# A long convolution and a mixture of experts on one core: x copied into the output in memory, the shared expert added by adding transfers, and shared and routed work in one ordered region

## The chip, the cores and the metric

The kernel runs on one core of a Trainium2 chip. A core has five engines that each work through a queue of their own: TensorE (PE, matrix products, with its weight loads listed apart as PEld), VectorE (DVE), ScalarE (ACT), GpSimd (POOL) and SyncE (SP, which here only issues transfers and waits). Transfers run on 16 DMA engines beside them, and an engine may issue transfers from its own queue. The metric is the time of one execution on the device in microseconds (us); of several runs the median is given. The trace gives spans of each instruction, and the page drawn from it also gives the clock that TensorE was granted.

## The reference

Two layers, all in single precision. A state-space layer makes a kernel of 512 taps for each of 32 heads, convolves each head of x (128 batch rows, 32 heads, 512 positions) with it causally, adds x times D and masks by the row's length. Its output goes to a mixture of experts with one shared expert, and x is added to the sum.

```python
def _L0_cond_ref(u, log_dt, C, log_A_real, A_imag, D, length):
    # K (32, 512) = 2 * Re(sum over 64 states of Ct * exp(dtA * l))
    K = _get_kernel(log_dt, C, log_A_real, A_imag, Lq)
    y = causal_convolution(u, K)          # written with rfft / irfft
    y = y + u * D[:, None]
    mask = (jnp.arange(Lq)[None, :] < length[:, None]).astype(u.dtype)
    return y * mask[:, None, :]

def _L0_ffn_ref(hidden_states, gate_w, bias, Wg, Wu, Wd, Sg, Su, Sd):
    x = hidden_states.reshape(-1, 512)                   # 4096 tokens
    scores = jax.nn.sigmoid(x @ gate_w.T) + bias         # 16 experts
    topk_w, topk_idx = jax.lax.top_k(scores, 4)
    topk_w = topk_w / (jnp.sum(topk_w, axis=-1, keepdims=True) + 1e-20)
    cw = jnp.sum(jax.nn.one_hot(topk_idx, 16) * topk_w[..., None], axis=1)
    z = silu(einsum('th,eih->eti', x, Wg)) * einsum('th,eih->eti', x, Wu)
    out = einsum('eti,ehi->th', z * cw.T[:, :, None], Wd)        # I = 256
    return out + silu(x @ Sg.T) * (x @ Su.T) @ Sd.T

x = x + ffn(cond(x, ..., lengths))      # lengths lie between 78 and 453
```

## The kernel before

The work runs in four stages. The first two are put in order by a scheduler, which decides from dependences and its own costs in which order each engine's queue gets its instructions; the last two are written out in the order in which they are to be issued.

*Making the convolution's kernels (0 to about 24 us).* Heads are handled in pairs, and the 16 pairs in four chunks, of 2, 4, 4 and 6 pairs. For a chunk, `waves` builds sines on ACT and exponentials on DVE and POOL: POOL makes `wv`, and DVE turns it into an exponential by a series (`exp_parts`, L244 to L251, on tiles `wv`, `wk`, `wq` of 192 columns for the second chunk). `kernels` then multiplies factors into `f_r`, `f_i`, `gg_r`, `gg_i` (DVE and POOL), a small product `pk` on PE sums over states, DVE adds D (`krow`, L392), SP writes `krow` to a scratch `kd` in memory (L399), and `kernel_strip` reads it back as `strip`, a Toeplitz matrix of 4 heads by 512 columns (L409; 1 MB, and for the first block four pieces of 256 KB). Only the first chunk also needs the tiles ct_r and ct_i, which all later ones use.

*Convolution (first product at 26.62 us, last gate product at 153.8).* There are NB = 8 blocks `tb` of HB = 4 heads. For each head `convolve` multiplies x's transposed block `xt` with the strip into `py` (four products, L512), DVE evacuates it under the length mask into `yb` (L519), PE transposes it into `pt` while ordering batch rows by length (L522), and ACT copies it to `yh` and to `yT` (L524 to L526). After each block a transfer in ACT's queue stores `yb` as rows of `y_rows` (L826), `gates` multiplies `yh` with the gate's weights (`pg`, L545), and after every second block `route` computes the routing on DVE; its last step is a product `cw_ps` on PE (L603), a copy to `cw_o` on ACT and a store (L606). The chunk of a later block is made two blocks ahead in program order, its strip one block ahead. SP loads `xt` for the next block and, at the start, the lengths (`len_col`, `len_row`).

*Shared expert (153.8 to 327.2 us).* `unit_step(u)` handles NU = 8 units of 512 tokens: 16 rows of neighbouring length by 32 heads. It computes g (`up`, L889), SiLU on ACT (L948), u (L889) and z on DVE (L951), twice, with 1 to 4 products of 128 positions as the lengths need; then `down` (L915) for the unit before, in four quarters of 128 tokens. POOL `fetch`es the rows of x for a quarter by an indirect transfer into `xg` (L903), DVE adds `o` to `xg` (L922), and POOL puts the rows into `out` by an indirect transfer (L924). Between these, `next(making)` takes one step at a time of `slots`, a generator that makes the tables of the routed tiles: counts (step 1), `nu_b` (2), `marks` and others (3), `pos`, `slot` and others (4), load tables (5), and then 16 groups of 8 one-hot pairs on DVE (`rows`, `cols`, L778 and L779) that PE sums into `pa` (L767). `unit_step(8)` has only the last `down`s. Once the tables are there, SP loads experts' weights into a ring of R = 8 places (`store`, 1.5 MB each, L840).

*Routed tiles (to the end).* Up to 143 tiles of 128 tokens of one expert. `turn_of(step)` gathers the tokens of a tile four ahead (POOL, L854), transposes them (`tokens`, L997, copied on ACT to `yt`, L1003), multiplies g and u (`inner`, L1029), makes z (L1040, L1041), transposes it (`turn`, L1047, L1050), multiplies down (`outer`, L1055), copies to `ob` (L1064, in the buffers `xg`) and adds the rows to `out` by an adding indirect transfer on POOL (L1065). `order` makes SP wait for all adds of the expert before when a new expert begins, since the same row may be added to.

Of the kernel before, what the change touches and what calls it, by code (L numbers as in the profile page):

```python
# [28 lines left out]
F32 = mybir.dt.float32  # L29
# [45 lines left out]
def ssm_moe_kernel(  # L75
# [459 lines left out]
    pgs = {}  # L535
# [17 lines left out]
    def route(rb):  # L553
# [46 lines left out]
        nc.vector.tensor_mul(cw, s, over_e(free))  # L600

        cw_ps = ps_m.tile([P, nh * E], F32, tag="m", name=f"cw_ps{rb}")
        nc.tensor.matmul(cw_ps, lhsT=to_row, rhs=flat(cw), start=True, stop=True)  # L603
        cw_o = stile("cw_o")
        nc.scalar.copy(flat(cw_o), cw_ps)
        nc.sync.dma_start(out=y_bh[:, hs, L:], in_=cw_o)  # L606
# [209 lines left out]
    for tb in range(NB):  # L816
        yb = yp.tile([P, HB, L], F32, tag="yb", name=f"yb{tb}")
        x_next = load_xt(tb + 1) if tb + 1 < NB else None
        for q in range(HB):
            convolve(tb, q, xb, yb)  # L820
            if tb * HB + q in chunk_at:
                c0, n = chunk_at[tb * HB + q]
                kernels(c0, n, *waves(c0, n, 0)[0])
            if q == 0 and tb + 1 < NB:
                kernel_strip(tb + 1)
        nc.scalar.dma_start(out=y_bh[:, tb * HB : (tb + 1) * HB, :L], in_=yb)  # L826
        gates(tb)
        if tb % RB == RB - 1:
            route(tb // RB)
        xb = x_next  # L830
# [47 lines left out]
    xg = homes(fp, "xg", [P, L], 6)  # L878
# [20 lines left out]
    def rows_of(u, q):  # L899
        return bass.IndirectOffsetOnAxis(ap=unit_rows[:, u, q : q + 1], axis=0)  # L900

    def fetch(u, q):
        nc.gpsimd.indirect_dma_start(  # L903
            out=at(xg, u * (TU // P) + q),
            out_offset=None,
            in_=x_rows,
            in_offset=rows_of(u, q),
        )

    def down(u, q):  # L910
        n = u * (TU // P) + q
        po, xq = at(p_o, n), at(xg, n)
        for it in range(IT):
            c0 = WD + it * L
            nc.tensor.matmul(  # L915
                po,
                lhsT=at(zu, u)[:, it, q * P : (q + 1) * P],
                rhs=w_sh[:, c0 : c0 + L],
                start=(it == 0),
                stop=(it == IT - 1),  # L920
            )
        nc.vector.tensor_add(xq, po, xq)  # L922
        nc.gpsimd.nop()
        put = nc.gpsimd.indirect_dma_start(  # L924
            out=out, out_offset=rows_of(u, q), in_=xq, in_offset=None
        )
        for other in adds:
            tc.declare_no_dep(put.ins, other.ins, reason="other rows")
        adds.append(put)
# [8 lines left out]
    def unit_step(u):  # L938
# [3 lines left out]
        if u < NU:  # L942
            fetch(u, 0)
            fetch(u, 1)
            k_us[u] = nc.tensor.value_load(k_u[0:1, u : u + 1], min_val=1, max_val=KT)
            for it in range(IT):
                up(u, it, p_g, 0)
                nc.scalar.activation(sgu[it], p_g[it], AF.Silu)  # L948
                next(making, None)
                up(u, it, p_u, I)  # L950
                nc.vector.tensor_mul(at(zu, u)[:, it, :], sgu[it], p_u[it])  # L951
                next(making, None)
        if u > 0:
# [31 lines left out]
    obs = xg[:3]  # L985
# [5 lines left out]
    def tokens(t):  # L991
# [9 lines left out]
        else:  # L1001
# [5 lines left out]
            texp[:, t : t + 1],  # L1007
# [11 lines left out]
    def registers(t):  # L1019
        w0s[t] = nc.tensor.value_load(  # L1020
            woff[0:1, t : t + 1], min_val=0, max_val=(R - 1) * WSZ
        )
        k_ts[t] = nc.tensor.value_load(ntk[0:1, t : t + 1], min_val=1, max_val=KT)
# [28 lines left out]
    def outer(t):  # L1052
        po = at(p_o, t)
        for it in range(IT):
# [12 lines left out]
            out_offset=bass.IndirectOffsetOnAxis(ap=put[:, t : t + 1], axis=0),  # L1067
# [9 lines left out]
    def order(t):  # L1077


        new = nc.sync.value_load(fresh[0:1, t : t + 1], min_val=0, max_val=1)  # L1080
        with tc.If(new > 0):
            wait = nc.sync.nop()
            for other in adds:
                dep(wait, other, "the rows they add to")
        marks[t] = nc.sync.nop()

    with tc.manual_schedule(engines=None):
        registers(0)

        def turn_of(step):  # L1090
# [26 lines left out]
        for step in range(NT_MIN + 2):  # L1117
            turn_of(step)

        def rest(step):  # L1120

            if step == NT + 2:
                return
            _, (some,) = nc.values_load_multi_w_load_instructions(
                full[0:1, step - 2 : step - 1], min_val=0, max_val=1
# [57 lines left out]
```

## Time and profile before

| | |
|---|---|
| Three runs | 965.4, 962.52, 962.6 us; median 962.6 |
| The profiled execution | 962.73 us, span of the trace 961.0 us |
| Mean granted TensorE clock | 0.986 |
| TensorE busy | 905.0 us, 94% of the span |
| VectorE, ScalarE, GpSimd busy | 426.6, 185.3, 431.2 us |
| First product of the convolution | 26.62 us |
| Last gate product / first product of the shared expert | 153.8 us |
| Last `down` of the shared expert ends | 327.2 us |

Busy times of different engines overlap, so they do not add up to the span: an engine that is busy 44% of the time costs nothing unless another waits for it. The table of windows gives, for a stretch of the span, the busy time of PE, PEld, DVE, ACT, POOL and SP with the number of instructions, then the granted clock, the mean busy share of the DMA engines and their GB/s. In the timeline a line gives start and length in us, the engine (SPq is SP's DMA queue), the line of the kernel, the operation with output and inputs, how many were taken together, and in brackets what ended an idle time before it.

### The profile page before, as it was taken

Reading aid. Unit: us, or ns where it says so; the run is one execution under the profiler, and the core shown is the slowest. Engines: PE = TensorE matmul, PEld = TensorE weight load, DVE = VectorE, ACT = ScalarE, POOL = GpSimd, SP = SyncE. Lnnn points to the kernel's source line nnn. Section 1 sums busy time; section 2 is a strip of 40 time slices with the busy share of each in tenths; the row PEclk is TensorE's granted clock in tenths of the full one; section 3 lists DMA queues with packets and bytes.
Section 4 is the critical chain, followed back from the end, with each engine's and each line's share of the span. In section 5 each row is a group of like instructions: output and inputs, shape, how many; then the busy total and the mean of one; then the engine's idle time right before and its main releaser. Section 6 shows DMA issues by size and latency. Waiting matters only on the chain.

```text
span 961.0 us, 14800 instructions
## 1 busy us (share of the span) xinstructions
PE 905.0 (94%) x3088; PEld 467.7 (49%) x3088; DVE 426.6 (44%) x1438; ACT 185.3 (19%) x367; POOL 431.2 (45%) x396
## 2 busy tenths in 40 slices
PE   0899998989998999999999999999999999999995
PEld 0567775434444444444444444444444544444442
DVE  7835555778762223342334233423433323334332
ACT  1133332000001012221222112211222212222221
POOL 3210002033455545564556555655555445556644
PEclk9999998999999999999999999999999999999998
DMA  4466653164456766777667766765766656667765
GB/s 160 138 214 197 205 175 114 43 251 146 165 197 192 252 157 113 126 141 160 113 119 139 166 113 116 140 107 110 123 125 113 113 90 113 113 116 138 131 111 104
DMA packets 53649, 135.96 MB, mean 141 GB/s; under 512 B 12400, under 2 KB 12560, under 8 KB 50960
## 3 DMA queue, kind: packets, MB, share of 16 engines
q0 software_dynamic: 35616, 89.77, 47.8%
q1 hardware_dynamic: 13680, 36.15, 11.2%
q10 hardware_dynamic: 4224, 8.39, 2.3%
q8 instruction: 72, 1.18, 0.5%
q14 instruction: 57, 0.47, 0.1%
HBM read 288.08 MB, written 52.25 MB: 354 GB/s over the span
## 4 chain that ended last, share of the span: by engine, by line
PE 85%; DVE 10%; issue 2%; another core or an unknown queue 1%; POOL 1%; ACT 0%; DMA 0%; SPq 0%; DVEq 0%; POOLq 0%
PE g L1029 34%; PE o L1055 24%; PE py L512 7%; PE m L997 4%; PE o L915 4%; PE u L1047 3%; PE pg L545 3%; PE u L889 2%; DVE cols L779 2%; PE pt L522 2%; PE g L889 2%; DVE rows L778 1%; DVE z L951 1%; DVE wq L251 1%
## 5 line engine op out<-in xcount | busy, mean ns | idle before, releaser
L1029 PE MATMUL g<-store,yt 128*128 x742 | 344.7, 598 | 4.4 <-ACT yt L1003 2.9
L1065 POOL DMA_INDIRECT out<-xg,put x134 | 212.1, 1583 | 238.5 <-DVE junk L1004 205.8
L1055 PE MATMUL o<-store,zT 128*128 x536 | 252.1, 593 | 0.0
L1041 DVE SCALAR_TENSOR_TENSOR zt<-g,wt,sgt 128x256 f32<-128x256 f32 x135 | 65.3, 483 | 290.2 <-ACT sgt L1040 284.0
L1029 PEld LDWEIGHTS g<-store,yt 128*128 128x128 f32 x742 | 130.9, 191 | 122.4 <-issue 118.0
L1055 PEld LDWEIGHTS o<-store,zT 128*128 128x128 f32 x536 | 101.4, 190 | 129.0 <-issue 124.6
L854 POOL DMA_INDIRECT yg<-y_rows,get x140 | 138.7, 991 | 42.6 <-issue 29.5
L1064 DVE COPY xg<-o 128x512 f32<-128x512 f32 x134 | 92.6, 691 | 108.8 <-PE o L1055 107.7
L1003 ACT COPY yt<-m 128x512 f32<-128x512 f32 x136 | 79.5, 585 | 234.8 <-PE m L997 220.7
L1040 ACT ACTIVATE sgt<-g 128x256 f32<-128x256 f32 x135 | 51.7, 383 | 273.4 <-PE g L1029 231.4
L512 PE MATMUL py<-strip,xt 128*128 128x512 f32 (+3 forms) x256 | 82.8, 460 | 4.9 <-DMA strip<-kd 4.9
L997 PEld LDWEIGHTS m<-ident,yg 128*128 128x128 f32 x373 | 48.6, 141 | 72.6 <-issue 72.6
L903 POOL DMA_INDIRECT xg<-in_x,unit_rows x32 | 31.1, 973 | 108.4 <-DVE sig_k L245 98.0
L924 POOL DMA_INDIRECT out<-xg,unit_rows x32 | 31.5, 984 | 93.3 <-DVE xg L922 86.0
L915 PE MATMUL o<-store,z 128*128 128x512 f32 x128 | 58.9, 609 | 6.1 <-DVE xg L922 6.1
L997 PE MATMUL m<-ident,yg 128*128 128x128 f32 x373 | 63.1, 273 | 1.2 <-issue 1.1
L1050 DVE COPY zT<-u 128x256 f32<-128x256 f32 x134 | 56.2, 419 | 0.1
L512 PEld LDWEIGHTS py<-strip,xt 128*128 128x128 f32 x256 | 44.0, 201 | 19.0 <-issue 8.3
L1047 PE MATMUL u<-ident,zt 128*128 128x128 f32 x268 | 51.3, 273 | 0.9 <-DVE zt L1041 0.9
L889 PE MATMUL g<-store 128*128 128x512 f32 x92 | 44.9, 625 | 0.0
L889 PE MATMUL u<-store 128*128 128x512 f32 x92 | 42.9, 601 | 0.7 <-issue 0.7
L915 PEld LDWEIGHTS o<-store,z 128*128 128x128 f32 x128 | 24.2, 195 | 37.1 <-issue 27.1
(267 smaller groups left out, 569.0 us busy)
## 6 DMA issues: line engine op xcount, KB each, us to landing
store<-in_w_all SPq DMA_DIRECT2D x143, 1536.0 KB
xt<-in_x_t SPq DMA_DIRECT2D x8, 1024.0 KB
y_rows<-yb ACTq DMA_DIRECT2D x8, 1024.0 KB
strip<-kd SPq DMA_DIRECT2D x7, 1024.0 KB
yg<-y_rows,get POOLq DMA_INDIRECT x140
out<-xg,put POOLq DMA_INDIRECT x134
strip<-kd SPq DMA_DIRECT2D x4, 256.0 KB
xg<-in_x,unit_rows POOLq DMA_INDIRECT x32
```

The source lines that it names most:

```text
L512: nc.tensor.matmul(py[:, : L - jt * P], lhsT=xt[:, jt, q, :], rhs=strip[tb][:, q, jt * P :], start=(jt == 0), stop=(jt == KT - 1),)
L854: nc.gpsimd.indirect_dma_start(out=at(yg, t), out_offset=None, in_=y_rows[:, :], in_offset=bass.IndirectOffsetOnAxis(ap=made["get"][:, t : ...
L889: nc.tensor.matmul(ps[it], lhsT=w_sh[:, c0 : c0 + P], rhs=yT[:, u, kt, :, :].rearrange("p h b -> p (h b)"), start=(kt == KT - n), stop=(kt ...
L915: nc.tensor.matmul(po, lhsT=at(zu, u)[:, it, q * P : (q + 1) * P], rhs=w_sh[:, c0 : c0 + L], start=(it == 0), stop=(it == IT - 1),)
L997: nc.tensor.transpose(pt[:, q, :], at(yg, t)[:, q * P : (q + 1) * P], ident)
L1003: nc.scalar.copy(at(yt, t), pt)
L1029: mm = nc.tensor.matmul(pgu, lhsT=at(yt, t)[:, q, :], rhs=ring_flat[:, bass.ds(w0s[t] + q * 2 * I, 2 * I)], start=(q == KT - n), stop=(q = ...
L1041: nc.vector.scalar_tensor_tensor(at(zs, t), pgu[:, I:], at(wts, t), sg, ALU.mult, ALU.mult)
L1047: nc.tensor.transpose(at(p_z, t)[:, it, :], at(zs, t)[:, it * P : (it + 1) * P], ident)
L1055: mm = nc.tensor.matmul(po, lhsT=at(zts, t)[:, it, :], rhs=ring_flat[:, bass.ds(w0s[t] + WD + it * L, L)], start=(it == 0), stop=(it == IT ...
L1064: nc.vector.tensor_copy(ob, po)
L1065: add = nc.gpsimd.indirect_dma_start(out=out, out_offset=bass.IndirectOffsetOnAxis(ap=put[:, t : t + 1], axis=0), in_=ob, in_offset=None, ...
```

## The change

x is no longer fetched and added in the shared expert. Instead eight transfers from memory to memory, one per block of the convolution and 1 MB each, copy x into `out` in ACT's queue (two added lines after the store of `yb`). `fetch` is gone; `down` copies its result to `ob` on ACT and adds it to `out` by an adding indirect transfer. The last step of `route` becomes `weights_out`; for the last pair of blocks it is called in `unit_step(0)` behind the products of that unit. `next(making)` is called after each z and after the second and fourth quarter of `down`, in unit 0 too, which has no `down`; before, it was called after each g and each z. Shared and routed stages stand in one ordered region, with `turn_of(0)` ahead of `unit_step(8)`. The routed tiles use the six `ob` buffers where they used three of `xg`, and their tables are looked up in `made` when they are wanted. Products and their shapes are the same in both kernels.

```diff
@@ -598,12 +598,19 @@
         nc.vector.reciprocal(free, tot)
         cw = stile("cw")
         nc.vector.tensor_mul(cw, s, over_e(free))
-
+        cws[rb] = cw
+
+    def weights_out(rb):
+
+
+        nh = RB * HB
         cw_ps = ps_m.tile([P, nh * E], F32, tag="m", name=f"cw_ps{rb}")
-        nc.tensor.matmul(cw_ps, lhsT=to_row, rhs=flat(cw), start=True, stop=True)
-        cw_o = stile("cw_o")
-        nc.scalar.copy(flat(cw_o), cw_ps)
-        nc.sync.dma_start(out=y_bh[:, hs, L:], in_=cw_o)
+        nc.tensor.matmul(
+            cw_ps, lhsT=to_row, rhs=cws[rb].rearrange("p h e -> p (h e)"), start=True, stop=True
+        )
+        cw_o = sp.tile([P, nh, E], F32, tag="cw_o", name=f"cw_o{rb}")
+        nc.scalar.copy(cw_o.rearrange("p h e -> p (h e)"), cw_ps)
+        nc.sync.dma_start(out=y_bh[:, rb * nh : (rb + 1) * nh, L:], in_=cw_o)
 
 
     def ctile(name, shape, dtype=F32):
@@ -824,9 +831,14 @@
             if q == 0 and tb + 1 < NB:
                 kernel_strip(tb + 1)
         nc.scalar.dma_start(out=y_bh[:, tb * HB : (tb + 1) * HB, :L], in_=yb)
+
+        own = slice(tb * P * HB, (tb + 1) * P * HB)
+        nc.scalar.dma_start(out=out[own, :], in_=x_rows[own, :])
         gates(tb)
         if tb % RB == RB - 1:
             route(tb // RB)
+            if tb + 1 < NB:
+                weights_out(tb // RB)
         xb = x_next
     conv.close()
     cst = ctx.enter_context(tc.tile_pool(name="cst", bufs=1))
@@ -875,7 +887,7 @@
 
     zu = homes(fp, "z", [P, IT, TU], 2)
     sgu = homes(fp, "sg", [P, TU], 2)
-    xg = homes(fp, "xg", [P, L], 6)
+    obs = homes(fp, "ob", [P, L], 6)
     p_g, p_u = homes(ps_g, "g", [P, TU], 2), homes(ps_u, "u", [P, TU], 2)
     p_o = homes(ps_o, "o", [P, L], 2)
     k_us, adds, loads = {}, [], []
@@ -896,20 +908,9 @@
 
         by_tiles(k_us[u], products)
 
-    def rows_of(u, q):
-        return bass.IndirectOffsetOnAxis(ap=unit_rows[:, u, q : q + 1], axis=0)
-
-    def fetch(u, q):
-        nc.gpsimd.indirect_dma_start(
-            out=at(xg, u * (TU // P) + q),
-            out_offset=None,
-            in_=x_rows,
-            in_offset=rows_of(u, q),
-        )
-
     def down(u, q):
         n = u * (TU // P) + q
-        po, xq = at(p_o, n), at(xg, n)
+        po, ob = at(p_o, n), at(obs, n)
         for it in range(IT):
             c0 = WD + it * L
             nc.tensor.matmul(
@@ -919,14 +920,18 @@
                 start=(it == 0),
                 stop=(it == IT - 1),
             )
-        nc.vector.tensor_add(xq, po, xq)
+        nc.scalar.copy(ob, po)
         nc.gpsimd.nop()
-        put = nc.gpsimd.indirect_dma_start(
-            out=out, out_offset=rows_of(u, q), in_=xq, in_offset=None
+        add = nc.gpsimd.indirect_dma_start(
+            out=out,
+            out_offset=bass.IndirectOffsetOnAxis(ap=unit_rows[:, u, q : q + 1], axis=0),
+            in_=ob,
+            in_offset=None,
+            compute_op=ALU.add,
         )
         for other in adds:
-            tc.declare_no_dep(put.ins, other.ins, reason="other rows")
-        adds.append(put)
+            tc.declare_no_dep(add.ins, other.ins, reason="other rows")
+        adds.append(add)
 
     def free_after(j):
 
@@ -940,22 +945,20 @@
 
         nonlocal gathered
         if u < NU:
-            fetch(u, 0)
-            fetch(u, 1)
             k_us[u] = nc.tensor.value_load(k_u[0:1, u : u + 1], min_val=1, max_val=KT)
             for it in range(IT):
                 up(u, it, p_g, 0)
                 nc.scalar.activation(sgu[it], p_g[it], AF.Silu)
-                next(making, None)
                 up(u, it, p_u, I)
                 nc.vector.tensor_mul(at(zu, u)[:, it, :], sgu[it], p_u[it])
                 next(making, None)
-        if u > 0:
-            for q in range(TU // P):
+        if u == 0:
+            weights_out(NB // RB - 1)
+        for q in range(TU // P):
+            if u > 0:
                 down(u - 1, q)
-        if u < NU:
-            fetch(u, 2)
-            fetch(u, 3)
+            if q % 2 == 1:
+                next(making, None)
         while "get" in made and gathered < AHEAD:
             gather(gathered)
             gathered += 1
@@ -964,15 +967,6 @@
             e = nc.sync.value_load(made["lexp0"][0:1, j : j + 1], min_val=0, max_val=E - 1)
             loads.append(load_expert(e, ring_flat[:, j * WSZ : (j + 1) * WSZ]))
 
-    with tc.manual_schedule(engines=None):
-        for u in range(NU + 1):
-            unit_step(u)
-    for _ in making:
-        pass
-    put, texp, woff, load, loff, lexp, ntk, fresh, full = (
-        made[t] for t in "put texp woff load loff lexp ntk fresh full".split()
-    )
-
 
     w0s, k_ts = {}, {}
 
@@ -982,7 +976,6 @@
     sgs = homes(gp, "sgt", [P, I], 2)
     zs = homes(gp, "zt", [P, I], 2)
     zts = homes(gp, "zT", [P, IT, P], 2)
-    obs = xg[:3]
     p_t, p_gu = homes(ps_m, "m", [P, KT, P], 2), homes(ps_g, "g", [P, 2 * I], 2)
     p_z = homes(ps_u, "u", [P, IT, P], 2)
 
...
@@ -1085,6 +1078,10 @@
         marks[t] = nc.sync.nop()
 
     with tc.manual_schedule(engines=None):
+        for u in range(NU):
+            unit_step(u)
+        for _ in making:
+            pass
         registers(0)
 
         def turn_of(step):
@@ -1106,15 +1103,17 @@
             if 1 <= step < NT:
 
                 t = step - 1
-                e = nc.sync.value_load(lexp[0:1, t : t + 1], min_val=0, max_val=E - 1)
-                to = nc.sync.value_load(loff[0:1, t : t + 1], min_val=0, max_val=(R - 1) * WSZ)
-                go = nc.sync.value_load(load[0:1, t : t + 1], min_val=0, max_val=1)
+                e = nc.sync.value_load(made["lexp"][0:1, t : t + 1], min_val=0, max_val=E - 1)
+                to = nc.sync.value_load(made["loff"][0:1, t : t + 1], min_val=0, max_val=(R - 1) * WSZ)
+                go = nc.sync.value_load(made["load"][0:1, t : t + 1], min_val=0, max_val=1)
                 ld = load_expert(e, ring_flat[:, bass.ds(to, WSZ)], go)
                 for other in loads:
                     tc.declare_no_dep(ld.ins, other.ins, reason="another place of the ring")
                 loads.append(ld)
 
-        for step in range(NT_MIN + 2):
+        turn_of(0)
+        unit_step(NU)
+        for step in range(1, NT_MIN + 2):
             turn_of(step)
 
         def rest(step):
...
```

More of the change, by code (lines that the diff above doesn't have):

```diff
@@ L534, in ssm_moe_kernel @@
     choice = const.tile([P, H, E], F32, tag="choice", name="choice")
-    pgs = {}
+    pgs, cws = {}, {}
     def gates(tb):
@@ L1006, in tokens @@
             epos,
-            texp[:, t : t + 1],
+            made["texp"][:, t : t + 1],
             at(yg, t)[:, L:],
@@ L1020, in registers @@
         w0s[t] = nc.tensor.value_load(
-            woff[0:1, t : t + 1], min_val=0, max_val=(R - 1) * WSZ
+            made["woff"][0:1, t : t + 1], min_val=0, max_val=(R - 1) * WSZ
         )
-        k_ts[t] = nc.tensor.value_load(ntk[0:1, t : t + 1], min_val=1, max_val=KT)
+        k_ts[t] = nc.tensor.value_load(made["ntk"][0:1, t : t + 1], min_val=1, max_val=KT)
     def inner(t):
@@ L1066, in outer @@
             out=out,
-            out_offset=bass.IndirectOffsetOnAxis(ap=put[:, t : t + 1], axis=0),
+            out_offset=bass.IndirectOffsetOnAxis(ap=made["put"][:, t : t + 1], axis=0),
             in_=ob,
@@ L1077, in order @@
     def order(t):
-        new = nc.sync.value_load(fresh[0:1, t : t + 1], min_val=0, max_val=1)
+        new = nc.sync.value_load(made["fresh"][0:1, t : t + 1], min_val=0, max_val=1)
         with tc.If(new > 0):
@@ L1124, in rest @@
             _, (some,) = nc.values_load_multi_w_load_instructions(
-                full[0:1, step - 2 : step - 1], min_val=0, max_val=1
+                made["full"][0:1, step - 2 : step - 1], min_val=0, max_val=1
             )
```

## The prediction

> **What bounds the kernel now.** I read the page first (its engine row and the row of forty slices), then the table of windows, then the timelines of PE and of SP's queue around every place where PE has a hole, and last the order in which the two built programs put each engine's instructions.
>
> ```profile
> PE 905.0 (94%) x3088; PEld 467.7 (49%) x3088; DVE 426.6 (44%) x1438; ACT 185.3 (19%) x367; POOL 431.2 (45%) x396
> PE   0899998989998999999999999999999999999995
> ...
> 75.00:100.00 25.00, 24.98 (x145) 18.68 (x145) 11.49 (x41) 8.28 (x15) 0.00 (x0) 1.00 0.75 250
> 150.00:175.00 25.00, 21.55 (x67) 10.94 (x67) 14.58 (x63) 4.46 (x7) 6.10 (x6) 0.86 0.36 108
> 175.00:200.00 25.00, 20.68 (x47) 8.73 (x46) 21.19 (x63) 1.20 (x3) 1.99 (x2) 0.93 0.44 171
> 400.00:600.00 200.00, 199.45 (x613) 97.90 (x612) 72.01 (x216) 42.02 (x87) 112.81 (x88) 1.00 0.70 134
> ```
>
> PE is the bound, and the routed tiles (330 us to the end) are packed: 199.45 of 200 us. Nothing in the change shortens a matmul, so all it can win or lose lies in PE's holes before 330 us: the start, the convolution (to 153.8) and the shared expert.
>
> ```profile
> 21.96 0.32 SPq L399 DMA_DIRECT2D kd<-krow  x1
> 23.36 1.76 SPq L409 DMA_DIRECT2D strip<-kd  x4
> 34.38 0.33 SPq L399 DMA_DIRECT2D kd<-krow  x1
> 35.92 0.38 SPq L409 DMA_DIRECT2D strip<-kd  x1
> ```
> ```profile
> 26.62 4.63 PE L512 MATMUL py<-strip,xt 128*128 128x512 f32 x8 [4.94 <-DMA strip<-kd]
> ...
> 43.09 2.75 PE L545 MATMUL pg<-gw,yh 128*128 128x16 f32 x24
> 45.69 2.05 PE L512 MATMUL py<-strip,xt 128*128 128x512 f32 x2
> ...
> 153.80 5.93 PE L889 MATMUL g<-store 128*128 128x512 f32 x8
> 159.57 3.60 PE L889 MATMUL u<-store 128*128 128x512 f32 x8
> ...
> 196.46 5.10 PE L915 MATMUL o<-store,z 128*128 128x512 f32 x8 [4.32 <-DVE xg L922]
> ...
> 311.07 5.40 PE L1029 MATMUL g<-store,yt 128*128 x8 [2.88 <-ACT yt L1003]
> ```
>
> The reader is to see two chains. At the start, DVE's small operations end in `krow` (21.7 us), SP writes `kd`, loads the strip, and PE starts 4.9 us after `krow`. The second block's strip leaves at 35.92, ten microseconds before PE wants it (45.69). In the shared expert, 153.8 to 327.2 (173.4 us), work is 312 matmul records at 0.43 us = 134 us, one-hot sums 16 x 0.5 = 8, small products 1.6, two tiles' transposes 1.9 and one tile's `inner` 3.4: 149 us. So 24.4 us are holes or slow clock: 2.7 us before `cw_ps`, 4.3 before the first `down`, 2.9 at 308, slow matmuls after each (5.93, 5.10, 5.40 against 3.44 to 3.6), and about 2 us in each unit.
>
> **The change part by part.**
>
> *Fetches removed, x copied, adding transfers.*
>
> ```profile
> L1065 POOL DMA_INDIRECT out<-xg,put x134 | 212.1, 1583 | 238.5 <-DVE junk L1004 205.8 <-issue 18.9 <-DVE zT L1050 9.8
> ...
> L1003 ACT COPY yt<-m 128x512 f32<-128x512 f32 x136 | 79.5, 585 | 234.8 <-PE m L997 220.7 <-issue 10.4 <-PE o L1055 3.6
> ...
> L903 POOL DMA_INDIRECT xg<-in_x,unit_rows x32 | 31.1, 973 | 108.4 <-DVE sig_k L245 98.0 <-issue 9.1 <-DMA out<-xg,unit_rows 1.3
> L924 POOL DMA_INDIRECT out<-xg,unit_rows x32 | 31.5, 984 | 93.3 <-DVE xg L922 86.0 <-issue 4.3 <-DVE rows L778 3.0
> ...
> L922 DVE TENSOR_TENSOR xg<-o,xg 128x512 f32<-128x512 f32 x32 | 21.6, 688 | 29.8 <-PE o L915 23.8 <-DMA xg<-in_x,unit_rows 3.3 <-DMA yg<-y_rows,get 2.0
> ```
>
> POOL loses 32 fetches (31.1 us) and its 32 puts become adds, 984 to 1583 ns by the row of the routed adds (+19.2): 12 us less on an engine that is 45% busy. DVE loses 21.6 us; ACT gains 32 copies at 585 ns (18.7 us) where it was busy 1.2 to 1.8 of 25 us. None is on PE's path; what I credit is the wait `down` had for DVE. The first add must wait for all eight copies of x; the last is issued near the convolution's end, and the first add comes some 38 us after it (below), so it is hidden. Without that cover it would delay only `ob` buffers, of which there are six.
>
> *Unit 0 and the weights (`weights_out`).* The last `cw_ps` no longer stands between u and g of unit 0: the 2.7 us go. But the new order puts slots' steps 3 and 4 into a unit that has no `down`: PE stands while DVE makes `nu_b` and then `marks`. Ups of unit 0 end 16.3 us after the gates (5.9 + 3 x 3.44); z and step 2 on DVE take 1.9 us (0.69 + 1.1), step 3 another 1.9: about 3.5 us of new hole, and 1.6 of slow clock after it, by the row at 196.46. Steps 4 and 5 (11.6 and 4.9 us on DVE) then run under 14 us of ups and 7 of downs of real work: the 4.3 us hole with its 1.6 goes. One-hots at spread points: a group of eight is 3.1 us on DVE, and PE puts 3.4 to 5.2 us between points, so they stay hidden; 0.5 us a unit won over five. The merged region takes `turn_of(0)` before the last downs, so `yt` is copied under 6.9 us of matmuls: 2.9 + 2 won. Sum: -2.7 -5.9 -2.5 -4.9 +5.1 = -11; from the holes that stay (register loads, 1 us a unit) I trust three quarters: **-8 us**, bounds -3 and -14.
>
> *What moves in the convolution.* The diff does not touch it, but the order does. With copies of x in ACT's queue the built program has another DVE order: before `krow` of the first chunk now stand the exponentials of the second chunk and part of the third. By the profile's intervals: 3 x 0.26 + 3.43 us (L244 to L251 on 192 columns), 0.8 waiting for POOL's `wv`, 1.45 for five of chunk three, 0.45 for two more, and the real chain with ct_r and ct_i after them: `krow` 12.15 us after the point where both orders agree (16.75), not 4.97. **+7.2 us**. A copy of x is also ACT's first instruction, waiting for nothing. SP's `len_col` reuses its semaphore, so it waits until that megabyte has landed, and DVE waits for `len_col`; the first logs share the DMA engines with it. No row shows a copy from memory to memory. Low end 0 (DVE wants `len_col` at 8.5, issued 4.9); high end 5, at half the 333 GB/s (250 at a share of 0.75) for both directions. I take 2.
>
> *The second strip.* In the new DVE order all four evacuations of block 0 (L519) stand before `f_r` and `g` of chunk two, and on SP the load of x block 2, which waits for PE's last `py` of block 0, stands before `kd`. So it is serial: PE starts at 26.6 + 9.2 = 35.8; four heads 11.9; evacuation 0.9; `f_r` to `gg_i` 2.6 (27.40 to 29.96 before); `pk` 1.0; `krow` and issue 0.7; 1.5 to the strip's issue (34.38 to 35.92). That is 54.4. Landing: the trace shows 3.3 us for 256 KB (23.36 to 26.62); 768 KB more at 333 GB/s make 5.6. The Trainium skill (DMA: Bandwidth & Descriptors, "Anatomy of one DMA") would give 2.0 us plus bytes at 436 GB/s, 4.4 for a megabyte; this row is for software descriptors and gives 2.6 for the 256 KB that took 3.3, so the row decides; the sum would be 1.2 less. Another copy of x is issued just before; +1. PE restarts at 61 instead of 45.7: +15.3, less 1 of gates and transposes done meanwhile.
>
> *The clock.* Eight records after the hole ahead of 153.80 took 5.93 us against 3.60, after work with 16 columns. The skill (TensorE: Matmul & The Clock Gate, "What's actually happening") says that an idle window of about 3.4 us halves the clock and as long a busy one restores it, 1.7 us lost; it speaks against this change, whose new hole is some 7 us. The rows say 1.6 to 2.3: +2.
>
> *Further in the convolution.* `py` of block 3 now follows `py` of block 2 without transposes between: 8.7 us for a load of x and a strip that can leave only when block 1 is done; 2 MB take 2 + 6.3. Block 6 likewise. +1 (0 to 6). At the end six heads of transposes are left over and ACT's 1.2 us a head sets the pace: +1. Sum of the convolution: 15.3 - 1 + 2 + 1 + 1 = **+18 us** (11 to 26).
>
> Total: 962.7 (span 961.0 and 1.7 around it; the runs' median is 962.6) + 18 - 8 = **973 us**.
>
> **The rivals.** (a) *Copies collide (12%).* Eight megabytes read and written in the convolution, whose DMA share is already 0.75 at its fullest; strips are late in more than one block. For: 64 KB pieces share the engines with strips. Against: strips are loaded a block ahead. Two more stalls of 4 us and a slower start of 4: 985. (b) *The shared expert gives back more than the convolution loses (6%).* Place: PE's 24.4 us of holes from 153.8 to 327.2. If nearly all go (-21) and the strip lands at its low end (+12): 954. It decides once the shared expert runs under 173.4 - 18 = 155 us. For: DVE is relieved there. Against: steps 3 and 4 make a hole, register loads stay. (c) *They cancel (8%):* +13 and -13, 963. (d) *The reordering does not act:* not possible on DVE, whose queue is in order.
>
> **How the numbers follow.** 973 us, 74%, its own range 966 to 980; (a) 12%, (b) 6%, (c) 8%. 0.3% (2.9 us) is about what a measurement of this kernel can tell from none. The main case lies above 965.6 almost wholly, with (a): slower 0.86; (c) same 0.08; (b) faster 0.06. The range, 964 to 984, leaves out (b), most of (c) and half of (a).
>
> **What would show it.** Right: `krow` near 31 us; the first `py` near 36; `kd<-krow` of chunk two after the last `py` of block 0; a hole of 5 us or more on PE before block 1 and slow matmuls after it; gates ending near 172; a hole of 3 us after unit 0's ups; the shared expert in about 165 us; the tiles unchanged at 199 of 200. Wrong: a second strip issued before block 0 ends, a first add that PE waits for, or holes among the routed tiles.

## The result and the profile after

The changed kernel takes 989.1 us (median of six runs, 982.7 to 990.4), the kernel before 963.5 in runs beside it: 1.0245 times, interval 1.0224 to 1.0266. 973 was predicted, 964 to 984 the range. The direction was right, the size was not: 25.7 us between the profiled spans (986.7 and 961.0), where +10 was forecast.

The rows of the page of the changed kernel that answer to those of before:

```profile
PE 919.0 (93%) x3088; PEld 485.2 (49%) x3088; DVE 405.6 (41%) x1406; ACT 201.2 (20%) x399; POOL 416.7 (42%) x364
...
PE   0569999989999999999999999999999999999994
...
PEclk9959698799999999999999999999999999999997
```

The clock row of the kernel before:

```profile
PEclk9999998999999999999999999999999999999998
```

PE has as many products as before and is busy 14 us longer. That is not more work: the clock row shows it, with 5, 6, 8 and 7 among the first eight slices, where before had one 8. SP's queue and PE's row of the same kernel, by start and length in us:

```profile
2.71 3.83 SPq L112 DMA_DIRECT2D aim<-in_a_imag  x1
...
32.55 0.32 SPq L399 DMA_DIRECT2D kd<-krow  x1
33.96 1.76 SPq L409 DMA_DIRECT2D strip<-kd  x4
50.54 0.33 SPq L147 DMA_DIRECT2D xt<-in_x_t  x1
54.79 0.33 SPq L399 DMA_DIRECT2D kd<-krow  x1
59.42 3.41 SPq L409 DMA_DIRECT2D strip<-kd  x2
```
```profile
37.63 6.25 PE L512 MATMUL py<-strip,xt 128*128 128x512 f32 x10 [5.36 <-DMA strip<-kd]
...
60.61 0.32 PE L384 MATMUL pk<-f_r,gg_r 128*32 128x32 f32 x2 [6.18 <-DVE gg_r L377]
...
62.28 6.58 PE L545 MATMUL pg<-gw,yh 128*128 128x16 f32 x30
68.70 6.07 PE L512 MATMUL py<-strip,xt 128*128 128x512 f32 x10
...
109.17 3.44 PE L545 MATMUL pg<-gw,yh 128*128 128x16 f32 x16
...
190.69 5.25 PE L901 MATMUL g<-store 128*128 128x512 f32 x8
...
206.27 0.49 PE L608 MATMUL cw_ps<-cw,to_row 128*128 128x128 f32 x2
...
211.37 5.16 PE L901 MATMUL g<-store 128*128 128x512 f32 x8 [0.52 <-issue]
```

The two chains of the prediction stand there. The first `krow` leaves 10.6 us later (32.55 against 21.96), PE starts 11.0 later, the second chunk's `kd` waits until block 0 is done, and `py` of block 1 starts at 68.70. But the convolution ends at 190.69, 36.9 us later than before, not 18. The table of windows of the changed kernel (length, busy time of the engines with counts, then clock, share of the DMA engines, GB/s) shows what else there is:

```profile
55.00:60.00 5.00, 0.00 (x0) 0.00 (x0) 4.55 (x16) 1.80 (x4) 2.03 (x5) 0.50 1.26 442
65.00:70.00 5.00, 5.00 (x21) 4.48 (x21) 0.00 (x0) 0.00 (x0) 0.00 (x0) 0.50 0.84 274
...
110.00:115.00 5.00, 5.00 (x23) 4.70 (x23) 1.83 (x8) 1.15 (x3) 0.00 (x0) 0.50 0.01 3
...
125.00:130.00 5.00, 5.00 (x29) 3.75 (x29) 2.25 (x9) 1.62 (x3) 0.00 (x0) 1.00 1.17 462
...
425.00:625.00 200.00, 199.58 (x613) 97.96 (x612) 72.50 (x220) 42.33 (x88) 112.22 (x88) 1.00 0.70 134
```

55 to 60 is the hole. At 110 to 115 PE is never idle and still has half its clock. Transfers do not explain that: the DMA engines are idle there, and at 125 to 130 they are as busy as anywhere while the clock is 1.00. The trace's record of the clock has only the values 1.00 and 0.50. In the convolution of the changed kernel it is at 0.50 from 53.9 to 74.4, 98.3 to 115.4, 156.3 to 163.2 and, across its end, 180.2 to 193.9 us; in the kernel before from 45.7 to 49.1, 107.2 to 110.6 and, across its end, 151.5 to 158.4. The routed tiles are as packed as before.

A ledger puts a number on each. For windows of 1 us I take as idle the length less PE's busy time, as clock lost the busy time times (1 - clock), and the rest as work. "Convolution" is from the first `py` to the first g of the shared expert, "shared" from there to the first `outer`, "tiles" the rest of the span; all in us.

| | first py | convolution | idle | clock lost | work | shared | idle | clock lost | work | tiles |
|---|---|---|---|---|---|---|---|---|---|---|
| before | 26.6 | 127.2 | 3.3 | 4.3 | 119.6 | 176.0 | 14.1 | 5.4 | 156.5 | 631.2 |
| after | 37.6 | 153.1 | 10.3 | 24.4 | 118.4 | 162.2 | 5.3 | 3.1 | 153.8 | 633.8 |

So the 36.9 us by which the convolution ends later are 11.0 of later start, 7.0 of idle PE and 20.1 of slow clock, less 1.2 of work. The shared expert gave back 13.8, the end took 2.6.

### The profile page after: what moved, and what is told of

Same layout as the page of the kernel before. It is cut to its first block, busy times and chain, and to the rows that moved or that the text cites. A ratio compares the mean times of both kernels' runs of the same rounds, so it can differ in the third digit from the quotient of the medians.

```text
span 986.7 us, 14746 instructions
## 1 busy us (share of the span) xinstructions
PE 919.0 (93%) x3088; PEld 485.2 (49%) x3088; DVE 405.6 (41%) x1406; ACT 201.2 (20%) x399; POOL 416.7 (42%) x364
## 4 chain that ended last, share of the span: by engine, by line
PE 63%; issue 1%; SPq 0%; POOL 0%; DVE 0%; ACT 0%; POOLq 0%
PE g L1022 33%; PE o L1048 23%; PE m L990 4%; PE u L1040 3%; PE o L916 1%; POOL out L1058 0%; SPq L1123 0%; POOL yg L866 0%; SPq L1073 0%; SPq L1107 0%; SPq L1106 0%; DVE zt L1034 0%; SPq L1108 0%; ACT sgt L1033 0%; SPq L852 0%
## 5 line engine op out<-in xcount | busy, mean ns | idle before, releaser
L1058 POOL DMA_INDIRECT out<-ob,put x134 | 211.3, 1577 | 242.4 <-DVE junk L997 203.3
L1057 DVE COPY ob<-o 128x512 f32<-128x512 f32 x134 | 92.7, 692 | 109.7 <-PE o L1048 106.2
L925 POOL DMA_INDIRECT out<-ob,unit_rows x32 | 49.9, 1559 | 207.9 <-DVE rows L785 146.7
L512 PEld LDWEIGHTS py<-strip,xt 128*128 128x128 f32 x256 | 46.7, 207 | 29.8 <-issue 19.9
L519 DVE TENSOR_TENSOR yb<-py,within 128x512 f32<-128x512 f32 x32 | 21.8, 685 | 57.1 <-PE py L512 45.9
L545 PEld LDWEIGHTS pg<-gw,yh 128*128 128x128 f32 x256 | 43.1, 258 | 1.8 <-issue 1.6
L545 PE MATMUL pg<-gw,yh 128*128 128x16 f32 x256 | 42.4, 309 | 0.0
```

Source lines behind the costliest of these rows:

```text
L512: nc.tensor.matmul(py[:, : L - jt * P], lhsT=xt[:, jt, q, :], rhs=strip[tb][:, q, jt * P :], start=(jt == 0), stop=(jt == KT - 1),)
L545: nc.tensor.matmul(pg[:, n * E : (n + 1) * E], lhsT=y_head[h][:, lt, :], rhs=gw[:, lt, :], start=(lt == 0), stop=(lt == KT - 1),)
L1057: nc.vector.tensor_copy(ob, po)
L1058: add = nc.gpsimd.indirect_dma_start(out=out, out_offset=bass.IndirectOffsetOnAxis(ap=made["put"][:, t : t + 1], axis=0), in_=ob, in_offse ...
```

## The experiments

The first theory, "order", is that the scheduler's other order costs all of it; its rival, "traffic", that 8 MB of copies do. Four groups of runs were made; the kernel before had medians of 965.8, 964.9, 959.0 and 960.0 us in them. Times are therefore compared within a group or by the ratio to before, and differences of a few us by the stages of the profiled executions. Each group ran on another chip, and the kernel before moved by 0.7% between them, so two ratios from different groups do not settle a difference of that size either.

**Copies behind unit 0 (e1) and no copies (e2).** The copies leave the convolution:

```diff
-        nc.scalar.dma_start(out=out[own, :], in_=x_rows[own, :])
...
     with tc.manual_schedule(engines=None):
-        for u in range(NU):
+        unit_step(0)
+        for tb in range(NB):
+            own = slice(tb * P * HB, (tb + 1) * P * HB)
+            nc.scalar.dma_start(out=out[own, :], in_=x_rows[own, :])
+        for u in range(1, NU):
             unit_step(u)
```

> The eight copies of x are issued in the ordered region, behind unit 0, still in ACT's queue; the rest is the changed kernel. The built order of PE in the convolution is then that of the kernel before, and DVE's nearly. Theory 'order' (the scheduler's other order in the convolution costs the time): first py near 26.6 us, gates end near 154, the shared expert keeps what it won, total 950 to 953 us. Rival 'traffic' (8 MB read and written beside other transfers cost the time): the loss moves with the copies into the shared expert, whose adds and one-hots wait; the convolution ends near 154 but the total stays at 970 or more.

> As the kernel with the copies behind unit 0, but x is not copied at all: the output lacks the term x, and the adds do not wait for copies. Order: the same as with the copies behind unit 0 within 2 us (950 to 953), since the copies are hidden there. Traffic: faster than that kernel by 10 us or more.

e1: 953.0 us, ratio 0.987 (0.985 to 0.989); e2: 953.9, ratio 0.989 (0.987 to 0.991). The convolution of e1 is that of before to the tenth (127.2, idle 3.3, clock lost 4.3), by PE's rows:

```profile
26.63 4.63 PE L512 MATMUL py<-strip,xt 128*128 128x512 f32 x8 [4.90 <-DMA strip<-kd]
...
153.83 5.96 PE L898 MATMUL g<-store 128*128 128x512 f32 x8
```

Moving eight lines of issue by one stage turns 2.5% of loss into 1.3% of gain, and behind unit 0 the copies cost nothing that can be seen (e2, without them, is no faster). As it stands this speaks for "order"; it does not show yet what traffic inside the convolution would do.

**Copies alone (e3).** The kernel before with the two lines of the copy added, and nothing else.

> The kernel before with nothing added but the eight copies of x behind the stores in the convolution (fetch, DVE add and put are kept, the puts overwrite the copied rows). Its built order in the convolution is that of the changed kernel. Order or traffic: first py near 37.6 us, gates end near 190, total 963.5 + 37 = 1000 us, plus or minus 3. If instead the later calls of weights_out or the other stages made the loss in the convolution: first py near 26.6 and 964 to 968.

1008.9 us, ratio 1.046 (1.042 to 1.050): the copies alone make the loss, and more of it. First `py` at 37.02, convolution 159.0 (idle 24.0, clock lost 16.1, work 118.9). By the profiled execution (1002.9 us, the fastest of the four) the convolution is 5.9 us longer than in the changed kernel. The largest new wait in it is that of `cw_ps` of the last pair of blocks, still inside the convolution here, which stood 11.3 us for DVE's `cw`. So in the new order `weights_out` was probably worth more than the prediction's 2.7 us; it was not tried alone.

**Copies in SP's queue behind each store (e4).** `nc.sync` in place of `nc.scalar`, and a wait on the store of yb:

```diff
-        nc.scalar.dma_start(out=out[own, :], in_=x_rows[own, :])
+        cp_x = nc.sync.dma_start(out=out[own, :], in_=x_rows[own, :])
+        tc.add_manual_dep(cp_x.ins, st_y.ins.name, SYNC, reason="behind the store")
```

> The changed kernel with each copy of x in SP's queue and made to wait for its block's store of yb: all 8 MB still move during the convolution, from block 1 on. The built order is that of before up to the third block (chunks, strips, evacuations); from the fourth block on PE ends each block with its last transposes and gates before the next block begins. Order: gates end at 155 to 161 us, total 952 to 959. Traffic: strips come late in most blocks, gates end at 170 or later, total 967 to 990.

1003.0 us, ratio 1.039 (1.037 to 1.042). The expectation failed, and not mainly by traffic. PE's waits from 75 to 170 us (total, times, longest):

```profile
PE cw_ps L608 <- DVE cw L600: 22.1, 3, 10.7
PE py L512 <- DMA strip<-kd: 9.6, 1, 9.6
```

In this order `cw_ps`, which needs DVE's whole routing, stands ahead of the next block's `py`, and SP's load of the next `xt` and strip stands behind the store of `cw_o`. I had looked only at PE's blocks, not at what stood at their seams. As a test of traffic it decides nothing.

**One copy ahead (e6).** e1 with copy 0 put first in the program.

> The kernel with the copies behind unit 0, but the first copy is put ahead of everything in ACT's queue, as it stands in the changed kernel. The built order then has krow of the first chunk behind parts of later chunks, as in the changed kernel, but the second chunk's krow still ahead of block 0's evacuations, and PE's order is nearly that of before. Theory: the start alone costs 10 to 11 us and is not caught up: first py near 37, gates end near 164.5, total 963 to 964. Rival: the start's delay is made up later, since PE waits less in block 0: 955 to 958.

962.3 us, ratio 0.997 (0.996 to 0.998), against e1's 0.987: 1.0%, 10 us. PE starts at 37.07 and the convolution ends at 162.02, 8.2 later than in e1, since PE idles 2.2 us less in it. PE's and SP's rows of e6:

```profile
37.07 6.47 PE L514 MATMUL py<-strip,xt 128*128 128x512 f32 x12
```
```profile
2.71 3.29 SPq L112 DMA_DIRECT2D aim<-in_a_imag  x1
```

The start's term is shown: about 8 to 10 us. By the rows DVE reaches L306, the last point at which the orders agree, 3.0 us late (15.19 against 12.20): `logs` lands later beside the copy, and `len_row_i` is issued later, because SP's issue of `aim`, ahead of it, takes 3.3 us (3.83 in the changed kernel, 0.43 before, with no copy ahead of it). The rest is DVE's order.

**Narrow and wide products (e7, e8).** e1 with extra products between unit 6 and unit 7, whose result nobody reads:

```diff
+            if u == 6:
+                idle = ps_m.tile([P, 512], F32, tag="m", name="idle")
+                for _n in range(96):            # e8: 24
+                    nc.tensor.matmul(idle[:, :16],    # e8: 512 columns
+                        lhsT=w_sh[:, :P], rhs=w_sh[:, P : P + 16],
+                        start=True, stop=True)
```

> The kernel with the copies behind unit 0 and, behind unit 6, 96 extra products of 128 columns of weights with 16 moving columns, back to back, whose result nobody reads. At the 0.115 us of the gates (2.75 us for 24) they are 11 us. Theory 'narrow work lowers the clock': the granted clock falls to 0.5 within some 5 us though PE never waits; about 17 us, and the wide products behind it start slow (+2). Rival 'only waiting lowers it': 11 us at clock 1.00.

> As the kernel with the extra narrow products, but with 24 extra products of 512 moving columns in their place (24 x 0.43 = 10.3 us). Both theories: 10.3 us at clock 1.00, and the products behind it at full speed.

The row of the extra products and the one after it, and two windows of 3 us, of e7; then the row of e8:

```profile
288.24 38.52 PE L1087 MATMUL idle<-store 128*128 128x16 f32 x192
326.61 3.76 PE L898 MATMUL g<-store 128*128 128x512 f32 x4
```
```profile
288.00:291.00 3.00, 3.00 (x27) 2.76 (x26) 0.00 (x0) 0.59 (x1) 2.69 (x2) 0.99 1.00 126
291.00:294.00 3.00, 3.00 (x16) 3.00 (x16) 0.00 (x0) 0.00 (x0) 0.32 (x1) 0.50 0.98 140
```
```profile
286.68 20.76 PE L1087 MATMUL idle<-store 128*128 128x512 f32 x48
```

Each product is two records, so both expected times are half of what they should be (96 products at full clock are 192 x 0.107 = 20.6 us, 24 wide ones 48 x 0.43 = 20.6). Read so, the two theories part clearly. The wide products took their 20.8 us at clock 1.00. The narrow ones brought the clock to 0.50 within 3 us, with PE busy all the time, and kept it there for the rest of 38.5 us; the wide ones behind them lost 2.7 us (3.76 + 2.74 against 2 x 1.88). Each is one execution, but the two differ by far more than the kernel does from run to run. Long runs of products with 16 moving columns lower the clock by themselves, without a wait; transposes (`pt`) and `pk` were not tried alone.

**Bunched order, start and second strip in time (e12).** The changed kernel with an edge that keeps each copy behind its store in ACT's queue, without a wait (`NoSync` in place of e4's `SYNC`, `nc.scalar` kept).

> The changed kernel with each copy of x ordered behind its block's store of yb in ACT's queue. The built order is that of the kernel before up to block 1 (krow, second strip, interleaved gates), but from block 2 on PE does four to six heads of py in a row and then four heads of transposes and gates in a row, as in the changed kernel; all 8 MB move in the convolution. Theory 'bunched narrow work halves the clock': first py near 26.6, second strip in time, clock 0.5 in each bunch, gates end at 164 to 170, total 963 to 967. Rival 'start and second strip are the whole loss': gates end near 155, 953 to 955.

990.9 us, ratio 1.031 (1.028 to 1.034): far over the expectation. `py` starts at 27.0 and block 1 at 45.8, as before, and yet the convolution ends at 196.2: 169.2 long, idle 24.5, clock lost 25.6, work 119.2. Rows of e12:

```profile
83.36 5.81 PE L512 MATMUL py<-strip,xt 128*128 128x512 f32 x12 [4.47 <-DVE yb L519]
...
115.56 2.75 PE L545 MATMUL pg<-gw,yh 128*128 128x16 f32 x24
...
139.64 5.14 PE L545 MATMUL pg<-gw,yh 128*128 128x16 f32 x24
...
178.95 0.79 PE L608 MATMUL cw_ps<-cw,to_row 128*128 128x128 f32 x2 [6.95 <-DVE cw L600]
```

PE's waits from 27 to 197 us (total, times, longest):

```profile
PE py L512 <- DVE yb L519: 11.9, 4, 4.5
PE cw_ps L608 <- DVE cw L600: 9.4, 2, 7.0
PE py L512 <- DMA strip<-kd: 5.2, 1, 5.2
```

24 records of `pg` take 5.14 us at half clock and 2.75 where the clock still holds (115.56). Start and second strip are in time, and yet the convolution loses 42 us: half by clock, half by PE waiting at the bunches' ends for DVE, which evacuates and routes in bunches too. Some of the slow spells begin in or just behind such waits, so the two halves are not independent. The rival is out; my estimate of 10 to 16 us for the bunching was less than half. But this order is not that of the changed kernel, whose idle time behind block 1 is small, so 42 us is no share of its loss. The run also speaks on traffic: seven of the eight copies move inside the convolution, and the only wait of PE that ends on a transfer is the one for the first strip, as in the kernel before (4.9 us).

**Traffic in the order of before (e14).** The copies in SP's queue, four behind block 6's store and four behind block 7's.

> The changed kernel with the copies of x in SP's queue, four behind block 6's store and four behind block 7's; the built order of PE in the convolution is exactly that of before. 4 MB move beside block 7, 4 MB beside unit 0. Order: gates end near 154, ratio to before 0.987 (951 to 954). Traffic: the last strip and xt come late or PE slows in block 7, gates end at 158 or later, ratio 0.991 or more.

962.6 us, ratio 1.002 (1.001 to 1.004). The gates end at 156.66, but the 2.9 us were there at 109.68 already (106.30 before), ahead of any copy, and are clock (7.2 lost against 4.3); e10, which has no copy in its convolution either, shows the same there (130.0 us, 7.3 lost). The loss comes behind the convolution. SP's, ACT's and PE's rows:

```profile
147.81 24.60 SPq L838 DMA_DIRECT2D out<-in_x  x7
```
```profile
172.01 1.28 ACT L954 ACT_TABLE_LOAD   x1 [16.06 <-DMA y_rows<-yb]
```
```profile
181.36 0.16 PE L630 MATMUL pe<-reach,cnt 128*16 128x4 bf16 x1 [7.75 <-DVE free L598]
```

Seven copies share the engines with the last store of yb, ACT's first instruction of unit 0 waits for that store, and with SiLU late, z and everything behind it on DVE is late. Shared: 172.0 us, idle 12.5. So traffic has a price where a wait ends on a transfer beside it. In the convolution no wait of PE ended on a copy, but less of the traffic fell there than was intended: one copy at 131 us, the other seven only from 147.81 on.

**Points in unit 0 and spread points (e5, e10, e13).** e5 keeps small steps out of unit 0's end:

```diff
                 nc.vector.tensor_mul(at(zu, u)[:, it, :], sgu[it], p_u[it])
-                next(making, None)
-        if u == 0:
-            weights_out(NB // RB - 1)
-        for q in range(TU // P):
-            if u > 0:
+                if u == 1 and it == 0:
+                    weights_out(NB // RB - 1)
+                if u > 0 or it == IT - 1:
+                    next(making, None)
+        if u > 0:
+            for q in range(TU // P):
                 down(u - 1, q)
-            if q % 2 == 1:
-                next(making, None)
+                if q % 2 == 1:
+                    next(making, None)
```

> The kernel with the copies behind unit 0, with fewer small steps at unit 0's end: one step of slots in unit 0, none in its quarters, and weights_out and the next steps within unit 1, between products. There the hole behind unit 0's ups was 5.8 us with 1.6 us of slow clock after it (the row of g at 175.77, 5.25 us against 3.60). If that hole is DVE's small steps and the tail of route: 953 - 7 = 946 us, no hole over 1 us before the first down. If PE's stand is only moved into unit 1: 951 to 953.

950.9 us, ratio 0.986 (0.984 to 0.989): not told apart from e1 by time. By the stages 161.3 us against 162.9; the hole is gone, but PE now spends 2.4 us at the first one-hot group (211.06 to 213.48). e10 puts the points back behind each g and each z, e13 does so without copies:

> The kernel with the copies behind unit 0, with the steps of slots at the points of the kernel before (behind each g and each z, none in the downs). If the spread points cost by the hole behind unit 0 (5.8 us and 1.6 slow) and win 0.5 us a unit over five units, as the prediction has it: 950 to 951, with a smaller hole at unit 0. If the spread is what hides the one-hots: slower than 953, with PE waiting for DVE's rows and cols in units 1 to 4 (955 to 958).

> The kernel without copies of x (its output lacks x) with the steps of slots at the old points, behind each g and each z. In the kernel with copies ACT's issue of them took 29.83 us there and held SiLU; without them the points alone are seen. If the spread points win 0.5 us a unit but cost the hole behind unit 0, as predicted: 951 us or ratio 0.986. If PE then waits for DVE's rows and cols more than that: 956 to 959, ratio 0.992 to 0.996.

e10: 972.0 us, ratio 1.012 (1.009 to 1.015), by a cause that neither theory named. ACT's queue and PE:

```profile
177.19 29.83 ACTq L1080 DMA_DIRECT2D out<-in_x  x8
```
```profile
208.74 6.19 PE L913 MATMUL o<-store,z 128*128 128x512 f32 x8 [13.31 <-ACT ob L920]
```

The row runs from the first of eight issues to the last, each of 0.5 to 0.7 us. In this program four of the copies are held until semaphores of earlier transfers come (issued at 183.30, 192.66, 202.81 and 206.50 us), and SiLU and `ob` stand behind them in ACT's queue; in e1 the same eight issues took 5.13 us. e13 is free of that: 955.0 us, ratio 0.995 (0.993 to 0.997). Against e2 the ratios say 6 us slower, the two medians 1.1, the shared stages 1.8 (165.6 against 163.8). The hole behind unit 0 is smaller with the old points: the wait for `free` is 1.75 us and no slow product follows, while in e2 the waits there add up to 3.6 us and the g behind them takes 6.47 against 3.60. That is the price which the prediction put on the new points; they win it back and 1 to 2 us more, by the medians and the stages. The size is not settled, since the two runs stand in different groups.

**Downs ahead of turn_of(0) again (e9), and a better version (e11).** e9 calls `unit_step(NU)` first and then `turn_of` from step 0. e11 is e5 with one more point left out, behind the first z of unit 2.

> The kernel with the copies behind unit 0, with the last downs of the shared expert again ahead of turn_of(0), as in the kernel before. If the place of turn_of(0) hides the copy of yt: PE stands some 2.9 us ahead of the first inner and is slow for 2 us after it (rows 311.07 of before), so about 957 us. If the two ordered regions alone or nothing mattered: 953.

> The kernel with fewer steps at unit 0's end and one more point left out, ahead of the first one-hot group, where PE stood 2.4 us (rows of pa at 211.06 to 213.48): the first group has 5 us of products more to hide under. 948 to 949 us, ratio to before near 0.984; if the wait only moves to the first gather, which now comes one point later: 951.

e9: 952.6 us, ratio 0.993 (0.990 to 0.995); the shared stage is 162.9 us as in e1, and PE waits 0.33 us for `yt`. By time and by stage the place of `turn_of(0)` wins nothing (the ratio alone would say 5 us, across two groups). e11, on the same chip as e9: 947.9 us (946.2 to 949.4), 4.7 less than e9 and 1.2% under before (0.988; 0.985 to 0.991); shared 158.4, idle 2.3. It is the fastest of all, and faster than both kernels.

## Why the prediction was right or wrong

**Start: right.** +9.2 was said for the first `py`, +11.0 came, and e6 shows it alone. The 2 us given to the copy were 3.0, but not by `len_col`: SP's issue of `aim` was slow, and `logs` and `len_row_i` came late.

**Second strip: right in mechanism, 7.7 us too small.** Block 1 was to restart at 61 and did at 68.70, 23.0 later than before and not 15.3. 1.8 of it is the start. The strip could be issued only 4.6 us after `kd<-krow`, not 1.5, and `py` began 9.3 us after that issue, not 6.6. What shared the DMA engines then is on record: a megabyte of `xt` (50.54) and one of `yb`, issued just before, a copy of x (56.88), and the strip after, issued with it. How much of the 5.8 us belongs to the copy is not shown; a kernel with the changed order and without copies was not run. The hole of 6.2 us on PE has another cause: `pk` of the third chunk stood ahead of block 0's gates and waited for DVE's `gg_r`. PE then worked off these gates at half clock until the strip was there.

**Clock: the step that failed.** The prediction gave it +2: one hole, one slow spell behind it. It measured +20.1. By the ledger 4.4 of these fall ahead of block 1's restart, where PE had to wait for the strip in any case. The other 15.7 (20.0 against 4.3), with 0.9 more of idle PE and 2.7 less of work, make the 13.9 us by which the rest of the convolution is longer than before; with 1 us less for gates done ahead, 2 for the clock and 1 and 1 for loads and transposes, the prediction had 3 for it.

What the term left out is that runs of narrow products (16 to 128 moving columns here) lower the clock although PE does not wait. The rule of the Trainium skill (TensorE: Matmul & The Clock Gate, "What's actually happening"), that an idle window halves the clock, is not against the hole at 55 to 60 us (clock 0.50, though it fell at 53.9 already, half a us ahead of the hole), but the sum was made as if only waiting counted. e7 shows the other way: 16-column products at 100% busy PE brought the clock to 0.50. The traces of before say so already, by two rows of the prediction. In the kernel before PE is busy throughout around the `pg` of 43.09 us, and yet the two `py` records behind it take 2.05 us, about twice the 1.1 of such a pair at full clock:

```profile
45.00:50.00 5.00, 5.00 (x20) 3.38 (x20) 1.86 (x5) 1.38 (x3) 0.00 (x0) 0.66 0.90 293
```

And the "hole" ahead of the 5.93 us at 153.80 is a short wait between narrow products:

```profile
152.07 1.89 PE L545 MATMUL pg<-gw,yh 128*128 128x16 f32 x8 [0.67 <-ACT yh L524]
```
The order of before has `pg` of three heads in a row (24 records, 2.6 us), mostly with wide products on both sides; the clock fell at three of the eight such places, each time for 3.4 or 6.8 us. The new order ran `pt`, `pk` and `pg` of several heads in a row, for 9 us and more at 98 and at 181 us, without a wait, and there the clock stayed at 0.50 for 17.1 and 13.7 us (`pg` 3.44 us for 16 records at 109.17, against 2.75 for 24). I had written down that bunching ("follows without transposes between", "six heads of transposes are left over") and priced it by loads and by ACT's pace, +1 and +1.

**Shared expert: right in sum, partly for wrong reasons.** -8 was trusted, bounds -3 to -14; the stage gave -13.8. Right: the hole behind unit 0 (5.2 us with its small products, then 5.16 against 3.60), the end of the waits of `down` for DVE, a small net gain by the spread points (e13), hidden adds at 1559 ns (1583 estimated). Wrong: the wait for `yt` ends without `turn_of(0)` being moved (e9). What held SiLU for 10 us around 300 us in the kernel before, which the profile puts on an unknown queue, is gone in every kernel with one ordered region; that the joining does it was not tried alone.

**Tiles: nearly.** The last add is issued 12.3 us before the end of the span, 9.0 before (974.36 of 986.7, 952.00 of 961.0). Why was not tried.

**Rivals.** "Copies collide" gives 985, close to the measured time, but that is luck: it wanted strips late in several blocks, and in the changed kernel one was late. No `py` behind block 1 waits for a transfer, there or in e12 with seven copies beside it. What moved the order is the two added lines themselves (e3), and placing them behind unit 0 undoes it (e1).

## What to carry to other kernels

When a scheduler orders a stage, compare the order of all queues before and after, and price it at the seams: what stands ahead of the first wide product of the next block, and on which queue its load waits. Products with few moving columns should stay scattered among wide ones: at half clock a run of them costs twice its time and slows what follows. In these traces runs of 2.6 us brought that on at some places, runs of 9 us and more wherever they stood. Independent transfers that nobody needs soon belong in a region whose order is fixed, behind the work that they must not displace, and not ahead of compute on an engine that may have to wait for a semaphore to issue them.

## What the runs showed that was not expected

- 192 records of 16-column products halved the granted clock within 3 us at 100% busy PE, and held it at half for the 35 us that they went on.
- A row of windows can show a rate that is none. For the first copy of the changed kernel it gives 526 GB/s:

```profile
2.00:4.00 2.00, 0.00 (x0) 0.00 (x0) 0.00 (x0) 0.00 (x0) 2.00 (x15) 1.00 1.52 526
```

  A packet counts whole in the window in which it starts, as the share of 1.52 betrays. In the trace the sixteen packets of 64 KB start from 2.45 us on and the last ends at 6.40: 1 MB in 3.95 us, 265 GB/s. Until about then SP's issue of `aim` lasts (6.54), 3.83 us in place of 0.43.
- The same eight issues of copies took 5.13 us of ACT's queue in one program and 29.83 in another that differs only in where small steps are called.
